# Layer 0 of a four-layer cross-attention stack: keys and values by pairs of batches, scores by seven products of halves

## The chip, the core and the metric

The kernel runs on one core of a Trainium2 chip. The core has a matrix engine (TensorE, PE), a vector engine (VectorE, DVE), a scalar engine for activations (ScalarE, ACT), a general engine (GpSimd, POOL) and a sync engine (SyncE, SP), which here only issues DMAs. Each engine works through its own queue in order; semaphores tie them together. TensorE reads from SBUF and writes to PSUM, which has eight banks of 512 fp32 columns; GpSimd doesn't read PSUM in this kernel. PEld in a profile is the loading of TensorE's weights, which runs beside its matmuls. The metric is the device time of one execution in microseconds (us), the median of several runs.

## The reference

Four layers work on `x` of shape (4, 512, 512) with a context of shape (4, 64, 512): four batches `b`, 512 tokens, 512 channels. All is fp32. Layer 0, which most of the change concerns, is this (cut, names shortened; it has 16 heads of 128, and both attentions read the same context):

```python
def attention(q_in, ctx, wq, bq, wk, bk, wv, bv, wo, bo, bias_k, bias_v):
    qh = (q_in @ wq + bq).reshape(b, 512, 16, 128)
    kh = (ctx @ wk + bk).reshape(b, 64, 16, 128)
    vh = (ctx @ wv + bv).reshape(b, 64, 16, 128)
    kh = concatenate([kh, broadcast(bias_k)], axis=1)      # 65 keys
    vh = concatenate([vh, broadcast(bias_v)], axis=1)
    weights = softmax(einsum('bqhk,bthk->bhqt', qh, kh) / sqrt(128))
    return einsum('bhqt,bthk->bqhk', weights, vh).reshape(b, 512, 2048) @ wo + bo

x = x + attention(layer_norm(x, ln1), ctx, ...1)
x = x + attention(layer_norm(x, ln2), ctx, ...2)
h = layer_norm(x, ln_mlp)
x = x + gelu(h @ w_fc1 + b_fc1) @ w_fc2 + b_fc2            # 512 -> 2048 -> 512
```

Layer 1 is a small cross-attention. Layer 2 attends over its own 512 tokens and the 64 of the context (16 heads of 32), with an RMS norm and an MLP behind it. Layer 3 is a layer norm, a cross-attention over the context, a second layer norm and an MLP.

## The kernel before

**A plan makes the order.** The kernel doesn't issue its instructions as it describes them. Each `with pe(...)`, `dve(...)`, `act(...)`, `pool(...)`, `either(...)` or `load(...)` records one operation with an estimated cost for each engine that may do it; `either` allows ScalarE or VectorE, and `added` allows VectorE or GpSimd. `Plan.order` first merges streams that were declared to run side by side (`beside`) by their shares of TensorE time, then walks through time: each free engine takes the earliest recorded operation that is ready and has room in SBUF and PSUM, at most 150 us of TensorE work ahead of the oldest open operation (`AHEAD`; 60 us for loads). What it chooses becomes the fixed order of each engine's queue. Its estimates (`t_dve`, `t_act`, `t_pool`, `MM`, `TR`, and in `load` 5.0 us for each 2048 elements of a partition, in `attempt` 0.1 us for an issue on SP) decide this order; on the chip each instruction takes what it takes.

SBUF is one tile, "arena", PSUM one tile, "banks"; all buffers are cut from these two, so a profile names hardly anything else. Helpers record many operations under one line: `mm4` (L693) is any group of four matmuls, the evictions of `either` are at L546 and L547 (`move`), L551 and L552 (`shift`), L555 and L556 (`affine`), additions between SBUF buffers at L925 (`added`).

**Layer 0.** For each of its two attentions (`n`) and each half of the 16 heads (`half`), `l0_project` reads the weights of eight heads, four loads of 256 KB a head, and makes for all four batches at once: the keys `kT` and the values `vT` (L693, 256 context tokens wide), then `A`, the query weights times the keys (L788, 4 x 65 = 260 columns, `KW`), `cq`, the query bias times the keys (L794), and `U`, the values times the output weights (L807). The queries themselves are never made: the scores are the normalized tokens times `A`. Bias rows are made at L820 and L838.

`normed` makes the layer norm: statistics on VectorE (L712, L713), a square root on ScalarE (L718), the normalization itself on GpSimd (L725), transposes on TensorE (L734), and scale and offset as `affine`. `l0_attention` then takes one batch in four tiles of 128 tokens. A tile's scores for eight heads are eight matmuls of 128 x 260 (two banks); VectorE adds `cq` (L862), finds the maximum (L870) and subtracts it (L872), ScalarE takes the exponential (L874), VectorE sums (L877) and inverts (L879), GpSimd scales (L882, L884), TensorE transposes (L893) and multiplies by `U` (four matmuls 512 wide), and VectorE adds the result to `x` (L901). After the second half of the heads the bias rows are added (L906 to L917). L1656 adds the output bias row to `x` on GpSimd.

The loop over layer 0 takes `n`, then the first half for all four batches with the norm of each, then the second half for all four.

**The later layers.** Two batches at a time, an MLP (`mlp`) is declared beside the attention of another layer or pair, so that the plan mixes the two. The MLP already multiplies by seven products of halves instead of eight (`seven`, L963, with `moving_sums` and `stationary_sums`), as do projections of layers 2 and 3 (`token_sums`, `seven_halves`, L1241). `layer_norm` and `mean_of` (layer 3, and the RMS norm of layer 2) have their sums over channel chunks and the last product on GpSimd (L1312, L1341, L1344, L1357), a mean by a matmul (L1315, L1347), and a reciprocal of 3.3 us on VectorE (L1323).

Of the kernel before, what the change touches and what calls it, by code (L numbers as in the profile page):

```python
# [14 lines left out]
ALU = mybir.AluOpType  # L15
# [3 lines left out]
P = 128  # L19
# [9 lines left out]
KW = B * (T + 1)  # L29
F = 2048  # L30
# [166 lines left out]
class Plan:  # L197
# [174 lines left out]
    def attempt(self, narrow):  # L372
# [22 lines left out]
        while left:  # L395
            progress = True
            while progress:
# [8 lines left out]
                for e, heap in heaps.items():  # L406
# [58 lines left out]
                    if op.load:  # L465
                        free_at[e] = now + 0.1
                        dma_free = max(dma_free, now) + cost
                        end = max(dma_free, now) + 2.0
                        busy[e] += cost
                    else:  # L470
                        free_at[e] = end = now + cost
                        busy[e] += cost
                        heapq.heappush(events, (end, 0, -1))
# [144 lines left out]
def stack(nc, const, sbuf, psum, a, out):  # L618
# [56 lines left out]
    def load(view, src, n):  # L675
        with pl.op(load=True, SP=n / 2048 * 5.0) as o:
            o.dma_start(out=view, in_=src)
# [28 lines left out]
    def normed(src, scale, offset):  # L706
# [7 lines left out]
        rstd = sb(NT)  # L714
# [4 lines left out]
        with dve(4) as o:  # L719
            o.reciprocal(rstd.v(), rstd.v())  # L720
        xn = []
        for t in range(NT):
            n = sb(D)
            with pl.op(POOL=2.1) as o:
                o.tensor_scalar(  # L725
                    n.v(), src[t].v(), mv.v(NT, 2)[:, t, 0:1], rstd[:, t : t + 1], ALU.subtract, ALU.mult
                )
            xn.append(n)
# [15 lines left out]

    bias = {}

    def l0_project(n, half):
        A = [sb(HH * KW) for _ in range(NC)]
        cq = sb(HH * KW)
        U = [sb(HH // 2 * D) for _ in range(B)]  # L750
        if not half:

            bvd = sb(H * DH)
            with pool(512) as o:
                o.memset(bvd.v(), 0.0)
            for g in range(4):
                with pool(4) as o:
                    o.tensor_copy(
                        bvd[:, g * 129 : g * 129 + 109 : 36], col(f"L0_xattn_bias_v{n}")[:, 4 * g : 4 * g + 4]
                    )  # L760
            bias[n] = [bvd, sb(D), None]
        bvd, ub, _ = bias[n]
        vTs, wos = [], []
        for j in range(HH):
            h = half * HH + j
            heads = slice(h * P, (h + 1) * P)

            wk = loaded(chunks(a[f"L0_wk{n}"][:, heads]), NC, P)
            wq = loaded(a[f"L0_wqT{n}"][heads, :], D)
            kT = sb(KW)  # L770
            p = ps()
            with pe(4 * MM[256]) as o:
                mm4(o, p[:, : B * T], lambda c: wk.v(NC, P)[:, c, :], lambda c: ctxT[:, c, :])
            with either(256) as o:
                o.shift(kT.v(B, T + 1)[:, :, :T].k(0), p[:, : B * T].split(B, T), col(f"L0_xattn_bk{n}", h))
            with pool(1) as o:
                o.tensor_copy(kT.v(B, T + 1)[:, :, T].k(1), col(f"L0_xattn_bias_k{n}", h).to_broadcast([P, B]))
            wv = loaded(chunks(a[f"L0_wv{n}"][:, heads]), NC, P)
            vT = sb(B * T)
            p = ps()  # L780
            with pe(4 * MM[256]) as o:
                mm4(o, p[:, : B * T], lambda c: wv.v(NC, P)[:, c, :], lambda c: ctxT[:, c, :])
            with either(256) as o:
                o.shift(vT.v(), p[:, : B * T], col(f"L0_xattn_bv{n}", h))
            for c in range(NC):
                p = ps()
                with pe(MM[KW]) as o:
                    o.matmul(p[:, :KW], wq[:, c * P : (c + 1) * P], kT.v(), start=True, stop=True)  # L788
                with either(KW) as o:
                    o.move(A[c].v(HH, KW)[:, j, :].k(j), p[:, :KW])  # L790

            p = ps()
            with pe(MM[KW]) as o:
                o.matmul(  # L794
                    p[:, :KW], col(f"L0_xattn_bq{n}", h).to_broadcast([P, P]), kT.v(), start=True, stop=True
                )
            with either(KW) as o:
                o.move(cq.v(HH, KW)[:, j, :].k(j), p[:, :KW])
            wo = loaded(a[f"L0_wo{n}"][heads, :], D)
            vTs.append(vT)  # L800
            wos.append(wo)
            if j % 2:
                for b in range(B):
                    p = ps()
                    with pe(PAIR) as o:
                        for e in range(2):
                            o.matmul(  # L807
                                p[e * T : (e + 1) * T, :],
                                vTs[j - 1 + e][:, b * T : (b + 1) * T],
# [4 lines left out]
                    with either(D) as o:  # L814
                        o.move(U[b].v(HH // 2, D)[:, j // 2, :].k(j // 2), p.v())
            if j % 4 == 3:
# [16 lines left out]
        if half:  # L833
# [3 lines left out]
            with pe(MM[512]) as o:  # L837
                o.matmul(p.v(), fold, ub.v(), start=True, stop=True)  # L838
# [3 lines left out]
        return A, cq, U  # L842

    def l0_attention(n, half, b, hT, proj, pb):
        qs = 1.0 / math.sqrt(P)
        A, cq, U = proj
        for t in range(NT):

            p = ps(2)
            own = slice(b * (T + 1), (b + 1) * (T + 1))  # L850
            with pe(8 * MM[KW]) as o:
                for i in range(2):
                    mm4(
                        o,
                        p.v(2, 512)[:, i, :KW],
                        lambda c: hT[c][:, t * P : (t + 1) * P],
                        lambda c: A[c].v(HH, KW)[:, 4 * i : 4 * i + 4, own],
                    )
            sc = sb(HH * (T + 1))
            s3 = sc.v(HH, T + 1)  # L860
            with dve(520) as o:
                o.tensor_tensor(  # L862
                    sc.v(2, 4, T + 1),
                    p.v(2, 512)[:, :, :KW].arrange("p i (h s) -> p i h s", h=4),
                    cq.v(2, 4, KW)[:, :, :, own],
                    ALU.add,
                )
            m = sb(HH)
            with dve(520) as o:
                o.tensor_reduce(m.v(), s3, AX.X, ALU.max)  # L870
            with dve(520) as o:
                o.tensor_tensor(s3, s3, m.v().new(2).bc(P, HH, T + 1), ALU.subtract)  # L872
            with act(520, "exp") as o:
                o.activation(sc.v(), sc.v(), AF.Exp, scale=qs)  # L874
            r = sb(HH)
            with dve(520) as o:
                o.tensor_reduce(r.v(), s3, AX.X, ALU.add)  # L877
            with dve(8) as o:
                o.reciprocal(r.v(), r.v())  # L879
            pr = sb(HH * T)  # L880
            with pool(512) as o:
                o.tensor_tensor(pr.v(HH, T), s3[:, :, :T], r.v().new(2).bc(P, HH, T), ALU.mult)  # L882
            with pool(8) as o:
                o.tensor_tensor(  # L884
                    pb.v(NT, 2, 4, 4)[:, t, 0].arrange("p i g -> p g i")[:, 2 * half : 2 * half + 2, :].k((t, half)),
                    s3[:, :, T].arrange("p (g i) -> p g i", g=2),
                    r.v(2, 4),
                    ALU.mult,
                )
            p = ps()  # L890
            with pe(4 * TR) as o:
                for k in range(HH // 2):
                    o.transpose(p[:, k * P : (k + 1) * P], pr[:, k * P : (k + 1) * P], ident)  # L893
            prT = sb(HH * T)
            with either(512) as o:
                o.move(prT.v(), p.v())
            p = ps()
            with pe(4 * MM[512]) as o:
                mm4(o, p.v(), lambda k: prT[:, k * P : (k + 1) * P], lambda k: U[b].v(HH // 2, D)[:, k, :])
            with dve(512) as o:  # L900
                o.tensor_tensor(x[b][t].v(), p.v(), x[b][t].v(), ALU.add)  # L901
        if half:
# [12 lines left out]
            for t in range(NT):  # L915
                with dve(512) as o:
                    o.tensor_tensor(x[b][t].v(), banks[t].v(), x[b][t].v(), ALU.add)  # L917

# [389 lines left out]
    def mean_of(parts):  # L1308

        for i, j in ((0, 1), (2, 3), (0, 2)):  # L1310
            with pool(S) as o:
                o.tensor_tensor(parts[i].v(), parts[i].v(), parts[j].v(), ALU.add)  # L1312
# [22 lines left out]
    def layer_norm(src, scale, offset):  # L1335

        parts = []
        for i in range(2):
            t = sb(S)
            with pool(S) as o:  # L1340
                o.tensor_tensor(t.v(), src[2 * i].v(), src[2 * i + 1].v(), ALU.add)  # L1341
            parts.append(t)
        with pool(S) as o:
            o.tensor_tensor(parts[0].v(), parts[0].v(), parts[1].v(), ALU.add)  # L1344
# [10 lines left out]
        for c in range(NC):  # L1355
            with pool(S) as o:
                o.tensor_tensor(xc[c].v(), xc[c].v(), r.v(), ALU.mult)  # L1357
# [288 lines left out]
    for n in (1, 2):  # L1646
        hT, pb = [], []
        proj = l0_project(n, 0)
        row = load_row(f"L0_xattn_bo{n}")
        for b in range(B):  # L1650
            if n == 1:
                load_x(b)
            hT.append(normed(x[b], f"L0_xattn_ln{n}_scale", f"L0_xattn_ln{n}_offset"))
            for t in range(NT):
                with pool(512) as o:
                    o.tensor_tensor(x[b][t].v(), x[b][t].v(), row.v(), ALU.add)  # L1656
# [115 lines left out]
```

## Time and profile before

| | |
|---|---|
| median of 3 runs (lowest, highest) | 2810.38 us (2808.79, 2812.26) |
| the profiled execution: its time, its span | 2809.43 us, 2807.7 us |
| mean granted TensorE clock in it | 0.996 |
| TensorE idle in the span | 66 us |
| matmul records at L963 (MLPs): count, busy | 2688, 1214.6 us |
| records of the scores of layer 0 (128x260 at L693): count, busy | 1024, 232.8 us |
| records of keys and values from the context (128x256 at L693, all layers): count, busy | 640, 151.8 us |
| L725 on GpSimd: count, busy, mean | 48, 100.0 us, 2092 ns |
| loads of 256 KB of layer 0 weights: issue to landing | 3.1 to 3.8 us |
| HBM read, written | 123.52 MB, 4.19 MB |

A row of a profile's group list gives the line, the engine, the operation, what is written and read, the shape and the count, then the busy time, the mean of one instruction, and the idle time of the engine just before them with what ended it. A busy time is a union of spans, and a matmul's end is modelled, so it holds a little more than the engine's bare work. In a timeline a row begins with its start and its length; the last number of a row of waits is the longest one.

### The profile page before, as it was taken

Reading aid. Unit: us, or ns where it says so; the run is one execution under the profiler, and the core shown is the slowest. Engines: PE = TensorE matmul, PEld = TensorE weight load, DVE = VectorE, ACT = ScalarE, POOL = GpSimd, SP = SyncE. Lnnn points to the kernel's source line nnn. Section 1 sums busy time; section 2 is a strip of 40 time slices with the busy share of each in tenths; the row PEclk is TensorE's granted clock in tenths of the full one; section 3 lists DMA queues with packets and bytes.
Section 4 is the critical chain, followed back from the end, with each engine's and each line's share of the span. In section 5 each row is a group of like instructions: output and inputs, shape, how many; then the busy total and the mean of one; then the engine's idle time right before and its main releaser. Section 6 shows DMA issues by size and latency. Waiting matters only on the chain. (4 is left out here: it accounts for less than half of the span.)

```text
span 2807.7 us, 31089 instructions
## 1 busy us (share of the span) xinstructions
PE 2741.5 (98%) x10924; PEld 1566.2 (56%) x10924; DVE 1905.9 (68%) x3344; ACT 825.1 (29%) x1503; POOL 1073.0 (38%) x1136
## 2 busy tenths in 40 slices
PE   8999999999999999999999999999999989999999
PEld 6666666766655455555555655555454535454444
DVE  5646556556655577777786877778875878687655
ACT  1310112101221113552562355245332323232311
POOL 2720125301542352324335232423744556455521
PEclk9999999999999999999999999999999999999999
DMA  5112021120111120120102012011111111102210
GB/s 166 31 57 71 19 64 35 57 64 23 38 43 59 45 68 9 31 61 16 38 31 79 9 31 73 18 31 42 42 45 46 46 49 42 45 16 67 75 38 30
DMA packets 186523, 129.72 MB, mean 46 GB/s; under 512 B 6992, under 2 KB 163280, under 8 KB 186368
## 3 DMA queue, kind: packets, MB, share of 16 engines
q1 hardware_dynamic: 186000, 127.43, 15.0%
q8 instruction: 87, 1.43, 0.2%
q14 instruction: 68, 0.56, 0.1%
q0 software_dynamic: 80, 0.16, 0.0%
q10 hardware_dynamic: 288, 0.15, 0.0%
HBM read 123.52 MB, written 4.19 MB: 45 GB/s over the span
## 5 line engine op out<-in xcount | busy, mean ns | idle before, releaser
L963 PE MATMUL banks<-arena 128*128 128x512 f32 x2688 | 1214.6, 597 | 16.0 <-DVE arena L982 9.2
L925 POOL TENSOR_TENSOR arena<-arena 128x256 f32<-128x256 f32 (+1 forms) x579 | 597.8, 1046 | 658.7 <-DVE arena L547 108.9
L963 PEld LDWEIGHTS banks<-arena 128*128 128x128 f32 x2688 | 499.0, 191 | 593.2 <-issue 503.7
L693 PE MATMUL banks<-arena 128*128 128x260 f32 (+3 forms) x1968 | 598.4, 459 | 3.0 <-ACT arena L555 1.1
L693 PEld LDWEIGHTS banks<-arena 128*128 128x128 f32 x1968 | 358.5, 189 | 212.4 <-issue 169.7
L546 ACT COPY arena<-banks 128x512 f32<-128x512 f32 (+3 forms) x403 | 209.8, 543 | 751.8 <-PE banks L963 218.2
L925 DVE TENSOR_TENSOR arena<-arena 128x256 f32<-128x256 f32 (+1 forms) x465 | 374.4, 819 | 49.4 <-ACT arena L998 19.1
L547 DVE COPY arena<-banks 128x512 f32<-128x512 f32 (+3 forms) x513 | 292.4, 576 | 157.8 <-PE banks L963 48.0
L998 ACT ACTIVATE arena<-arena,cols 128x512 f32<-128x512 f32 x192 | 137.4, 721 | 394.9 <-DVE arena L982 175.3
L982 DVE TENSOR_TENSOR arena<-banks,arena 128x512 f32<-128x512 f32 x240 | 164.7, 686 | 120.5 <-PE banks L963 108.6
L882 POOL TENSOR_TENSOR arena<-arena 128x512 f32<-128x512 f32 x64 | 71.8, 1122 | 388.5 <-DVE arena L879 348.9
L1241 PE MATMUL banks<-arena 128*128 128x256 f32 x896 | 206.3, 380 | 2.6 <-DVE arena L982 1.0
L1470 ACT ACTIVATE arena<-banks,arena 128x512 f32<-128x512 f32 x256 | 174.7, 687 | 82.0 <-DVE arena L1460 38.6
L1241 PEld LDWEIGHTS banks<-arena 128*128 128x128 f32 x896 | 168.6, 190 | 54.1 <-issue 21.6
L1458 DVE TENSOR_REDUCE arena<-banks 128x1 f32<-128x512 f32 x256 | 167.3, 680 | 13.5 <-PE banks L1447 11.8
L1504 PEld LDWEIGHTS banks<-ident,arena 128*128 128x128 f32 x1024 | 115.3, 141 | 82.3 <-ACT arena L1470 30.2
L693 PE MATMUL banks<-ctxT,arena 128*128 128x256 f32 x640 | 151.8, 388 | 7.8 <-DMA arena<-in_L_wk 7.3
L1504 PE MATMUL banks<-ident,arena 128*128 128x128 f32 x1024 | 138.5, 276 | 9.6 <-ACT arena L1470 8.9
L693 PEld LDWEIGHTS banks<-ctxT,arena 128*128 128x128 f32 x640 | 121.9, 193 | 40.2 <-issue 12.7
L1021 DVE TENSOR_TENSOR arena<-banks,arena 128x512 f32<-128x512 f32 x144 | 98.4, 685 | 49.8 <-PE banks L963 49.4
L725 POOL TENSOR_SCALAR arena<-arena 128x512 f32<-128x512 f32 x48 | 100.0, 2092 | 30.6 <-DVE arena L720 12.4
L1481 POOL TENSOR_TENSOR arena<-arena 128x256 f32<-128x256 f32 x64 | 39.5, 617 | 187.1 <-DVE arena L1460 121.2
(152 smaller groups left out, 2437.6 us busy)
## 6 DMA issues: line engine op xcount, KB each, us to landing
arena<-in_L_w SPq DMA_DIRECT2D x192, 256.0 KB, 3.2
arena<-in_L_wk SPq DMA_DIRECT2D x48, 256.0 KB, 3.3
arena<-in_L_wqT SPq DMA_DIRECT2D x32, 256.0 KB, 3.7
arena<-in_L_wv SPq DMA_DIRECT2D x32, 256.0 KB, 3.6
arena<-in_L_wo SPq DMA_DIRECT2D x32, 256.0 KB, 3.1
arena<-in_L_wq SPq DMA_DIRECT2D x32, 256.0 KB, 3.8
arena<-in_L_wo SPq DMA_DIRECT2D x8, 1024.0 KB, 5.5
arena<-in_L_wv SPq DMA_DIRECT2D x6, 1024.0 KB, 7.3
```

Source lines behind the costliest of these rows:

```text
L546: "ACT": lambda e, out, in_: e.copy(out, in_),
L547: "DVE": lambda e, out, in_: e.tensor_copy(out, in_),
L693: o.matmul(dst, lhs(c), rhs(c), start=(c == 0), stop=(c == NC - 1))
L725: o.tensor_scalar(n.v(), src[t].v(), mv.v(NT, 2)[:, t, 0:1], rstd[:, t : t + 1], ALU.subtract, ALU.mult)
L925: o.tensor_tensor(out, x, y, op)
L963: o.matmul(p.v(), lhs(c), rhs(c), start=(c == 0), stop=(c == 1))
L982: o.tensor_tensor(t.v(), p.v(), y.v(), ALU.add)
L998: o.activation(g[f].v(), src.v(), func, bias=col(b1, q * NC + f))
L1241: o.matmul(p[:, i * 256 : (i + 1) * 256], lhs(c), rhs(c), start=(c == 0), stop=(c == 1))
L1458: o.tensor_reduce(m[:, i : i + 1].k(i), banks[i].v(), AX.X, ALU.max)
L1470: o.activation(y.v(), banks[i].v(), AF.Exp, bias=nm[:, i : i + 1].k(i), scale=qs, accum_out=sums[:, i : i + 1].k(i),)
L1504: o.transpose(p[:, c * P : (c + 1) * P], e[i][:, c * P : (c + 1) * P], ident)
```

## The change

- `l0_project` becomes `l0_keys` and `l0_values`, declared side by side, and both work for one pair of batches (`bp`; 128 context tokens, `KP` = 130 columns of keys). Each is therefore called for each pair, and each call loads the weights of its eight heads.
- The loop over layer 0 takes the pair first, then `n`, then the half of the heads. In the first half both batches of the pair are normed, then the output bias row is added to both, and then both are attended to.
- The scores of two tiles (tokens `m` and `2 + m` of the four) and eight heads are a product of 2 x 2 blocks: token halves by channel halves by head halves. It is made of seven block products instead of eight. `token_sums` makes the sums of the left side from the normed tokens, `l0_keys` those of the right side (`t1` to `t4`) and of the bias (`dcq`), and VectorE or GpSimd puts the blocks together. What follows for one tile is the new `l0_tile`, unchanged but for the subtraction of the maximum, which may now go to VectorE or GpSimd.
- In `normed` the normalization is a scale and an offset (`by`, one more small instruction) on ScalarE or VectorE instead of GpSimd.
- In `mean_of` and `layer_norm` the sums and the product on GpSimd may now go to VectorE or GpSimd (`added`).
- The plan's figure for a load is 3.15 instead of 5.0 us for 2048 elements, and an issue on SP is counted as 0.45 instead of 0.1 us.

```diff
-                        free_at[e] = now + 0.1
+                        free_at[e] = now + 0.45
...
-        with pl.op(load=True, SP=n / 2048 * 5.0) as o:
+        with pl.op(load=True, SP=n / 2048 * 3.15) as o:
...
+        with dve(4) as o:
+            o.scalar_tensor_tensor(by.v(), mv.v(NT, 2)[:, :, 0], -1.0, rstd.v(), ALU.mult, ALU.mult)
...
-            with pl.op(POOL=2.1) as o:
-                o.tensor_scalar(
-                    n.v(), src[t].v(), mv.v(NT, 2)[:, t, 0:1], rstd[:, t : t + 1], ALU.subtract, ALU.mult
-                )
+            with either(D) as o:
+                o.affine(n.v(), src[t].v(), rstd[:, t : t + 1], by[:, t : t + 1])
...
+    def l0_keys(n, half, bp):
+        tokens = slice(bp * P, (bp + 1) * P)
+        b11, b21, b22, t1, t2, t3, t4 = (sb(2 * 4 * KP).v(2, 4, KP) for _ in range(7))
+        cq, dcq = (sb(4 * KP).v(4, KP) for _ in range(2))
+        for j in range(4):
+            for e in range(2):
+                h = half * HH + 4 * e + j
+                heads = slice(h * P, (h + 1) * P)
+                wk = loaded(chunks(a[f"L0_wk{n}"][:, heads]), NC, P)
+                wq = loaded(a[f"L0_wqT{n}"][heads, :], D)
+                kT = sb(KP)
+                p = ps()
+                with pe(8 * TR) as o:
+                    mm4(o, p[:, :P], lambda c: wk.v(NC, P)[:, c, :], lambda c: ctxT[:, c, tokens])
...
+                made = []
+                for r in range(2):
+                    p = ps()
+                    with pe(4 * TR) as o:
+                        for c in range(2):
+                            o.matmul(p[:, c * KP : (c + 1) * KP], wq[:, (2 * r + c) * P : (2 * r + c + 1) * P], kT.v(), start=True, stop=True)
+                    made.append(p[:, : 2 * KP].split(2, KP))
...
+                if not e:
+                    for dst, p4 in ((b11, made[0]), (b21, made[1])):
+                        with either(2 * KP) as o:
+                            o.move(own(dst), p4)
...
+                with dve(2 * KP) as o:
+                    o.tensor_tensor(own(t1), own(b11), made[0], ALU.subtract)
+                with either(2 * KP) as o:
+                    o.move(own(b22), made[1])
+                with dve(2 * KP) as o:
+                    o.tensor_tensor(own(t3), own(b22), made[0], ALU.add)
+                added(own(t2), own(b22), own(t1), ALU.subtract, 2 * KP)
+                added(own(t4), own(b21), own(t2), ALU.subtract, 2 * KP)
...
+    def l0_attention(n, half, b, X, keys, U, pb):
+        for m in range(2):
...
+            u1 = plus(some(), product(a11, b11), cq[:, :, own])
+            u2 = plus(some(), product(s2, t2), u1)
+            u3 = plus(some(), product(s3, t3), u2)
+            p5 = plus(some(), product(s1, t1), dcq[:, :, own])
+            u4 = some()
+            added(u4, p5, u2, ALU.add, 2 * KP)
+            added(c22, p5, u3, ALU.add, 2 * KP)
+            plus(c11, product(a12, b21), u1)
+            plus(c21, product(a22, t4), u3)
+            plus(c12, product(s4, b22), u4)
+            for t, sc in ((m, scs[0]), (2 + m, scs[1])):
+                l0_tile(half, b, t, sc, U, pb, qs)
...
-            with pool(S) as o:
-                o.tensor_tensor(xc[c].v(), xc[c].v(), r.v(), ALU.mult)
+            added(xc[c].v(), xc[c].v(), r.v(), ALU.mult, S)
...
+    for bp, pair in enumerate(pairs):
+        for n in (1, 2):
+            X, pb = {}, {}
+            for half in range(2):
+                made = {}
+                pl.beside(
+                    lambda: made.update(keys=l0_keys(n, half, bp)), lambda: made.update(U=l0_values(n, half, bp))
+                )
+                if not half:
+                    row = load_row(f"L0_xattn_bo{n}")
+                    for b in pair:
+                        if n == 1:
+                            load_x(b)
+                        X[b] = token_sums(normed(x[b], f"L0_xattn_ln{n}_scale", f"L0_xattn_ln{n}_offset"))
...
+                for b in pair:
+                    l0_attention(n, half, b, X[b], made["keys"], made["U"], pb[b])
```

In `l0_attention` a `product` is two matmuls of 128 x 260 into one bank, and `plus` adds such a bank and a buffer on VectorE. `l0_values` makes `vT` (128 tokens), `U` for two batches and, for the first pair only, the bias rows, as before.

## The prediction, made before the changed kernel ran

> **What bounds the kernel now.** I read the busy shares first, then the busy times by stage, then the waits of TensorE, and last the timeline for single prices.
>
> ```profile
> PE 2741.5 (98%) x10924; PEld 1566.2 (56%) x10924; DVE 1905.9 (68%) x3344; ACT 825.1 (29%) x1503; POOL 1073.0 (38%) x1136
> ...
> 0.00:780.00 780.00, 769.62 (x3261) 518.28 (x3262) 453.28 (x854) 135.75 (x213) 240.86 (x279) 1.00 0.19 56
> 780.00:2808.00 2028.00, 1971.90 (x7665) 1047.94 (x7663) 1452.60 (x2491) 689.35 (x1291) 832.12 (x858) 0.99 0.14 42
> ...
> PE banks L693 <- DMA arena<-in_L_wk: 7.3, 1, 7.3
> PE banks L693 <- ACT arena L555: 1.1, 1, 1.1
> PE banks L693 <- DVE arena L556: 1.1, 1, 1.1
> PE banks L693 <- DVE arena L552: 0.6, 1, 0.6
> ```
>
> The columns of the two stage rows are TensorE, weight load, VectorE, ScalarE and GpSimd busy, then granted clock, DMA share and GB/s. Layer 0 is the first 780 us. TensorE is busy for 769.6 of them at full clock; the four waits below the rows are nearly all it waits for there, and 7.3 of them are the first load. So layer 0 costs what its matmuls cost, VectorE (58%) and GpSimd (31%) have room, and an edit counts by the TensorE time it removes or the waits it makes. After 780 us TensorE is idle for 56 us.
>
> **Prices.** Busy times overlap at the seams, so I take the distance from start to start in the timeline. An fp32 matmul leaves two records (the scores are 512 matmuls and 1024 records), a transpose one.
>
> ```profile
> 33.10 3.62 PE L693 MATMUL banks<-ctxT,arena 128*128 128x256 f32 x16
> 36.55 1.92 PE L788 MATMUL banks<-arena 128*128 128x260 f32 x8
> 38.30 0.60 PE L794 MATMUL banks<-arena,cols 128*128 128x260 f32 x2
> ...
> 92.18 0.60 PE L893 MATMUL banks<-ident,arena 128*128 128x128 f32 x4
> 92.62 1.54 PE L734 MATMUL banks<-ident,arena 128*128 128x128 f32 x12
> ...
> 1019.96 2.79 PE L693 MATMUL banks<-arena 128*128 128x64 f32 x24
> 1022.58 0.65 PE L963 MATMUL banks<-arena 128*128 128x512 f32 x1
> ```
>
> Eight matmuls 256 wide take 3.45 us (0.431 each), four 260 wide 1.75 (0.4375), twelve 64 wide 2.62 (0.218), four transposes 128 wide 0.44 (0.11 for one record).
>
> **The change, part by part.**
>
> Scores. Before: 64 tiles of 8 matmuls 260 wide, 512. After: 32 pairs of tiles with seven products of two, 448. The built order of the changed kernel has 448 too. 64 x 0.4375 = **28.0 us off TensorE**, nothing else of it being on the path.
>
> Keys and values by pairs of batches. 256 matmuls 256 wide become 512 that are 128 wide; the 128 + 32 of A and cq (260) become 256 + 64 that are 130 wide. The columns are the same, the instructions twice as many. No fp32 matmul of 128 columns is in this trace. Lower bound: half of the 256-wide one, 0.2156, which costs nothing more. Upper bound: the straight line from 64 (0.218) to 256 (0.431), 0.289 at 128 and 0.291 at 130, since a cost that is flat and then rises lies under its chord: 512 x 0.289 - 110.3 = 37.7, and 320 x 0.291 - 70.0 = 23.1, together +60.8. I take two records of 0.109, because the 64-wide matmul shows that a record with its weight load can't go below that, and the 128-wide transposes show that 128 columns with a weight load need no more: 512 x 0.2185 - 110.3 = +1.6 and 320 x 0.222 - 70.0 = +1.0, **+2.6 us**. The U products, bias rows and all transposes keep their number (the bias rows are made for the first pair only).
>
> Against this stands a page of the Trainium skill, "TensorE: Matmul & The Clock Gate", section "Back-to-back issue gap": a real stream of weight load and matmul at 128 columns is said to sustain about 81 ns each, where columns alone would give 56, a surcharge of some 45%. As an estimate from that page, 832 narrow matmuls would pay about 82 us more, and the sum would end near 2870. The row of 64-wide matmuls, each with its 128 x 128 weights, speaks against it.
>
> VectorE and GpSimd in layer 0. For a pair of tiles the old 2 x 0.696 (L862) becomes seven additions out of PSUM of 260 elements, 0.418 each by L1253 (256 wide): +1.53 us. Two sums of 260 in SBUF and the two subtractions of the maximum (0.780, L872) may now go to either engine. So a pair of tiles holds VectorE for 7 x 0.418 + 2 x (0.689 + 0.690 + 0.197 + 0.690) = 7.5 us, and 11.8 if it also took all that could go elsewhere (2 x 0.707, 2 x 0.780, 2 x 0.688 of moves). TensorE needs 14 x 0.4375 + 8 x 0.11 + 8 x 0.858 = 13.9. Projection: two heads take TensorE 16 x 0.2185 + 10 x 0.222, and 2 x 0.96 for U (four such pairs took 3.84 us, L807): 7.6 us, with the bias rows of the first pair 8.2. Moves, shifts, differences and sums take 6.6 us if VectorE does all. Both fit; value **0** while the planner's order keeps products ahead, and what it costs if that cover is gone is in the second rival. Token sums of layer 0 (64 additions of 256, 0.71 to 0.80) go beside attention. By the built order's counts VectorE gains about 41 us in layer 0 (453 to 494 of some 755) and GpSimd about 105.
>
> LayerNorm, `normed`. 48 GpSimd steps of 2.09 us become ScalarE or VectorE steps of about 0.72 to 0.81 (L998, L556); one small instruction is added for each. ScalarE is 17% busy in layer 0 (136 of 780), so the exponentials queued behind them wait little. On the path they stand only where a stage starts, in the two waits of 1.1 us: the first product stands at the head of TensorE's queue, and all that follows waits with it. There are now four such starts (two pairs, two attentions), and eight sums stand behind the last transposes. Three of the seven products need none of the sums, and in the built order 38 to 42 matmuls follow the transposes without a break. I take 1.5 us for each start, bounds 0.5 and 3: 4 x 1.5 - 2.2 = **+4** (0 to +10). The additions of the output bias (L1656) now stand behind both norms of a pair on GpSimd, and only the residual additions (L901) at the end of a tile need them.
>
> LayerNorm of layer 3 (`mean_of`, `layer_norm`): 92 GpSimd steps of 1.36 to 1.42 us may go to VectorE. Where such a norm is exposed, both engines are full:
>
> ```profile
> 2003.00:2044.00 41.00, 35.02 (x81) 15.26 (x80) 39.00 (x40) 19.26 (x26) 38.44 (x36) 0.92 0.00 1
> 2303.00:2331.00 28.00, 18.85 (x36) 7.43 (x35) 26.81 (x26) 13.69 (x19) 25.34 (x21) 0.82 0.00 0
> ```
>
> TensorE loses 15.1 us there, with a lower granted clock, but VectorE and GpSimd are over 90% busy, so moving a step between them frees little: **-1**. At best half of the 15 goes (-8); at worst steps of 0.945 us stand on VectorE ahead of the L982 that TensorE waits for, five times (+5).
>
> Loads. The 128 weight loads of layer 0 are issued twice: 33.5 MB and 128 issues on SP more. From 10 to 30 us the DMA engines moved 334 to 344 GB/s, all they do here. One stage's 32 loads are 8.39 MB, 24.7 us at 339 GB/s, under the 4 x 7.6 = 31 us of projection; an issue took 0.43 to 0.55 us, 16 for the 32. TensorE waited for a load once, before the first. Value **0**, nothing to gain, worst case in the third rival. The planner's new figures (0.79 us for 256 KB, an issue of 0.45) move no work by themselves; they reorder all later layers, where 56 us are idle: 0, and I allow 10 either way.
>
> Sum: -28.0 + 2.6 + 4 - 1 = -22.4 on the profiled execution's 2809.43 (span 2807.7), 2787.0. The median of the runs shown is 0.95 above that execution: **2788 us**. The forecast's own range takes the starts at 0 and +10, layer 3 at -8 and +5, and 5 us either way for the order: 2772 to 2805.
>
> **Rivals.**
> 1. Narrow matmuls pay for their weights. At the chord the sum is 2810.4 - 28.0 + 60.8 + 3 = 2846. It turns to a loss from (180.3 + 25) / 832 = 0.247 us each. Against it: the 64-wide row. Chance 0.04.
> 2. Stage starts take the gain back, slower than before. Behind the last tile of a pair stand statistics (4 x 0.87), a table load and root (1.28 + 0.2 and three small steps, 0.7), four normalizations on two engines (1.5), transposes (1.75), affine (0.8) and sums three deep (2.1): 11.8 us. Open at all four starts, with 2.2 known, that is +45 and 2829; it decides from (26.4 + 2.2) / 4 = 7.2 us a start. For it: a pair has half the other work that four batches had. Against it: 31 us of projection is independent and stands ahead of the transposes in the built order. Chance 0.08.
> 3. Loads come late: each of the seven later stages waits for one landing (3.1 to 3.8 us by the list of DMA issues), +24, so about 2812: no change. For it: buffers are shared, and SP already waits for them. Chance 0.10.
> 4. The later layers gain too: the 8 us of layer 3 and 10 from the new order, 2771. Chance 0.10.
> 5. That the products aren't fewer is excluded by the built order.
>
> **How the numbers follow.** The forecast has 0.68. Differences under 0.2%, 5.6 us, can't be told from none: faster is 0.68 + 0.10 = 0.78, within 0.2% 0.10, slower 0.12. The range 2768 to 2812 leaves out rivals 1 and 2 and a little at the lower end.
>
> **What would show it.** Scores 448 matmuls at 0.4375 from start to start and key matmuls near 0.219; layer 0 over near 758 us instead of 780; gaps before the first products of four stages of 1 to 3 us; VectorE in layer 0 near 65%. Wrong would be: 128-wide matmuls over 0.247, waits for DMA beyond the first one, or layers 1 to 3 shifted by more than 10 us.

## The result and the profile after

The changed kernel took a median of 2821.18 us (2819.88 to 2826.01, 5 runs) against 2810.05 us (2808.79 to 2812.26, 5 runs): ratio 1.0043, 95% interval 1.0029 to 1.0058. The forecast was 2788. The profiled execution took 2821.01 us with a span of 2819.2, 11.5 more than before.

Busy shares of the changed kernel, then its busy times by stage, with the columns as before:

```profile
PE 2742.9 (97%) x11628; PEld 1578.9 (56%) x11628; DVE 1968.8 (70%) x3569; ACT 885.8 (31%) x1659; POOL 1095.0 (39%) x1277
```

```profile
0.00:780.00 780.00, 764.01 (x3938) 525.61 (x3939) 496.51 (x1051) 194.54 (x371) 280.14 (x423) 1.00 0.33 100
780.00:2819.00 2039.00, 1978.85 (x7693) 1053.26 (x7691) 1472.29 (x2519) 691.28 (x1289) 814.82 (x854) 0.99 0.14 42
```

TensorE is as busy as before (2742.9 us against 2741.5), though 64 score matmuls are gone. The waits of TensorE in the changed kernel show little of where that went: between 25 and 760 us they come to 6.9 us, against 2.4 before. The longest of all and the longest of layer 0:

```profile
PE banks L1031 <- ACT arena L1423: 12.3, 2, 9.5
PE banks L694 <- DMA arena<-in_L_wk: 7.4, 1, 7.4
PE banks L977 <- ACT arena L547: 1.8, 3, 0.8
PE banks L785 <- DVE arena L553: 1.3, 1, 1.3
PE banks L735 <- ACT arena L552: 1.1, 1, 1.1
```

(L1031 is the product of the MLPs. From here on, layer 0 means its two attentions; its MLP counts with the later layers.) So I matched each record of TensorE with the operation that it belongs to, added up the distances from start to start, and charged what goes beyond the usual distance of a form to the record that came late. Split by the layer for which the work is done, the wait for the first load with layer 0:

| | layer 0 | later layers | span |
|---|---|---|---|
| before | 767.1 | 2040.6 | 2807.7 |
| changed | 768.9 (+1.8) | 2050.3 (+9.7) | 2819.2 |

Two things are to be explained: a layer 0 that gained nothing, and later layers that lost 9.7 us with hardly a change in their arithmetic.

**Where layer 0's gain went.** The timeline of TensorE in the kernel before, where a projection ends:

```profile
36.55 1.92 PE L788 MATMUL banks<-arena 128*128 128x260 f32 x8
...
38.84 3.84 PE L807 MATMUL banks<-arena 128*64 128x512 f32 x16
42.61 1.07 PE L820 MATMUL banks<-arena 128*32 128x512 f32 x8
43.60 2.64 PE L693 MATMUL banks<-ctxT,arena 128*128 128x256 f32 x11
```

and the same kind of place in the changed kernel (L785 is A, L694 keys and values, L796 `cq`, L850 U):

```profile
327.23 1.05 PE L694 MATMUL banks<-ctxT,arena 128*128 128x128 f32 x8
328.12 0.39 PE L796 MATMUL banks<-arena,cols 128*128 128x130 f32 x2
328.34 1.05 PE L694 MATMUL banks<-ctxT,arena 128*128 128x128 f32 x8
329.33 1.08 PE L850 MATMUL banks<-arena 128*64 128x512 f32 x4
330.34 1.16 PE L785 MATMUL banks<-arena 128*128 128x130 f32 x8
331.43 1.08 PE L850 MATMUL banks<-arena 128*64 128x512 f32 x4
332.44 0.49 PE L796 MATMUL banks<-arena,cols 128*128 128x130 f32 x2
```

The U products use 64 columns of the array (128*64). Before, 16 of their records stand in a row; now four stand alone between full 128*128 matmuls. Read the starts: eight key records take 0.89 us (327.23 to 328.12), but 0.99 when U follows (328.34 to 329.33); the eight A records between two U groups take 1.09. In layer 0 an entry costs 93 ns nearly every time, whether operands and bank had been ready for 140 ns or for over 2 us; the first and the last pair of U records take 480 and 529 ns instead of 430, and the matmul behind the last one comes 103 ns late. A visit to a narrow tile thus costs about 0.35 us beyond its work (of U's 128 pairs 64 took 430 ns before, and 10 after). None of it is idle time in the profile, since the modelled ends overlap. Between 25 and 760 us there were 22 visits before and 70 after. The Trainium skill has the rule in "TensorEngine Tiling (Array Packing)", section "Key Properties": changing the tiling mode drains TensorE. The traces agree that the change costs time and give it a size, which the page doesn't; that it is a drain they don't show.

The accounts of layer 0, before to changed, from distances from start to start:

| term | us |
|---|---|
| scores: 225.0 to 201.0 | -24.0 |
| keys, values, A and `cq`, by the usual distance of a group | +5.6 |
| 48 more visits, entry and exit: 48 x (93 + 103) ns | +9.4 |
| U's own records: 60.2 to 64.1 | +3.9 |
| groups that start less than 200 ns after their bank (or operand) came free: 36 before, losing 4.4 us; 48 after, losing 13.9 (a few are entries too, and those behind a score, 1.5 us more than before, are in the scores' row as well) | +9.5 |
| transposes of the attentions' norms: 17.1 to 15.1 | -2.0 |
| sum (measured: +1.8) | +2.4 |

### The profile page after: what moved, and what is told of

The parts are those of the page before. It is cut to its first block, busy times and chain, and to the rows that moved or that the text cites. A ratio compares the mean times of both kernels' runs of the same rounds, so it can differ in the third digit from the quotient of the medians.

```text
span 2819.2 us, 33561 instructions
## 1 busy us (share of the span) xinstructions
PE 2742.9 (97%) x11628; PEld 1578.9 (56%) x11628; DVE 1968.8 (70%) x3569; ACT 885.8 (31%) x1659; POOL 1095.0 (39%) x1277
## 5 line engine op out<-in xcount | busy, mean ns | idle before, releaser
L993 POOL TENSOR_TENSOR arena<-arena 128x256 f32<-128x256 f32 (+3 forms) x828 | 840.0, 1030 | 1119.9 <-ACT arena L547 202.3
L1031 PE MATMUL banks<-arena 128*128 128x512 f32 x2688 | 1212.9, 597 | 18.2 <-ACT arena L1423 12.3
L1031 PEld LDWEIGHTS banks<-arena 128*128 128x128 f32 x2688 | 499.7, 191 | 594.9 <-issue 509.6
L993 DVE TENSOR_TENSOR arena<-arena 128x512 f32<-128x512 f32 (+3 forms) x564 | 449.8, 813 | 69.7 <-ACT arena L1066 16.2
L547 ACT COPY arena<-banks 128x512 f32<-128x512 f32 (+4 forms) x464 | 227.5, 511 | 786.4 <-PE banks L1031 215.6
L548 DVE COPY arena<-banks 128x512 f32<-128x512 f32 (+2 forms) x420 | 253.7, 613 | 189.0 <-PE banks L1031 43.9
L694 PE MATMUL banks<-arena 128*128 128x512 f32 (+2 forms) x944 | 371.1, 542 | 2.3 <-DVE arena L548 0.9
L694 PEld LDWEIGHTS banks<-arena 128*128 128x128 f32 x944 | 167.8, 190 | 180.1 <-issue 167.5
L1050 DVE TENSOR_TENSOR arena<-banks,arena 128x512 f32<-128x512 f32 x240 | 164.4, 686 | 104.1 <-PE banks L1031 94.6
L906 PE MATMUL banks<-arena 128*128 128x260 f32 x896 | 208.5, 384 | 0.8 <-ACT arena L547 0.7
L1309 PEld LDWEIGHTS banks<-arena 128*128 128x128 f32 x896 | 170.0, 191 | 54.8 <-issue 23.2
L906 PEld LDWEIGHTS banks<-arena 128*128 128x128 f32 x896 | 164.7, 188 | 38.4 <-issue 5.8
L694 PE MATMUL banks<-ctxT,arena 128*128 128x128 f32 (+1 forms) x1152 | 164.1, 291 | 8.8 <-DMA arena<-in_L_wk 7.4
L694 PEld LDWEIGHTS banks<-ctxT,arena 128*128 128x128 f32 x1152 | 148.5, 194 | 27.5 <-issue 13.6
L1568 PE MATMUL banks<-ident,arena 128*128 128x128 f32 x1024 | 140.6, 278 | 12.1 <-ACT arena L1534 11.5
L1089 DVE TENSOR_TENSOR arena<-banks,arena 128x512 f32<-128x512 f32 x144 | 98.7, 686 | 46.0 <-PE banks L1031 45.7
L985 DVE TENSOR_TENSOR arena<-banks,arena 128x512 f32<-128x512 f32 x64 | 44.2, 690 | 117.0 <-PE banks L694 114.1
```

The lines of the kernel that those rows point to most:

```text
L547: "ACT": lambda e, out, in_: e.copy(out, in_),
L548: "DVE": lambda e, out, in_: e.tensor_copy(out, in_),
L694: o.matmul(dst, lhs(c), rhs(c), start=(c == 0), stop=(c == NC - 1))
L906: o.matmul(p[:, : 2 * KP], lhs(c), rhs(c, b % 2), start=(c == 0), stop=(c == 1))
L993: o.tensor_tensor(out, x, y, op)
L1031: o.matmul(p.v(), lhs(c), rhs(c), start=(c == 0), stop=(c == 1))
```

## The experiments

"Layer 0" and "later" are the sums explained above, from each run's profiled execution; that of e7 is 5.7 us longer than its median, that of e9 6.1 shorter. All ratios are to the kernel before.

| run | median us | ratio, 95% interval | layer 0 | later |
|---|---|---|---|---|
| e1_figures | 2834.89 | 1.0089 (1.0072, 1.0105) | 789.0 | 2044.2 |
| e2_norms | 2810.57 | 1.0006 (0.9997, 1.0016) | 770.4 | 2039.8 |
| e3_pairs8 | 2836.69 | 1.0099 (1.0084, 1.0114) | 791.4 | 2043.7 |
| e4_oldfig | 2822.08 | 1.0046 (1.0031, 1.0061) | 785.0 | 2035.0 |
| e5_oldest_bank | 2801.32 | 0.9967 (0.9954, 0.9979) | 765.7 | 2033.8 |
| e6_oldest_bank_before | 2784.18 | 0.9908 (0.9895, 0.9922) | 758.2 | 2024.1 |
| e7_slack | 2813.91 | 1.0018 (1.0008, 1.0027) | 769.7 | 2048.2 |
| e8_ahead140 | 2816.49 | 1.0024 (1.0014, 1.0034) | 768.5 | 2046.0 |
| e9_u_in_fours | 2812.00 | 1.0007 (0.9998, 1.0015) | 758.5 | 2045.7 |
| e10_fours_oldest | 2786.41 | 0.9921 (0.9908, 0.9935) | 755.9 | 2031.9 |
| e11_twos_oldest | 2788.14 | 0.9923 (0.9910, 0.9935) | 753.6 | 2030.4 |
| e12_ln3_gpsimd | 2816.52 | 1.0026 (1.0014, 1.0038) | 768.7 | 2045.7 |
| e13_figures_layer0 | 2805.79 | 0.9986 (0.9977, 0.9994) | 769.4 | 2035.7 |
| e14_twos_oldest_fig0 | 2780.38 | 0.9896 (0.9882, 0.9909) | 754.6 | 2023.5 |
| e15_e14_ln3_gpsimd | 2784.86 | 0.9919 (0.9906, 0.9933) | 753.1 | 2030.0 |
| e16_issue_kept | 2805.65 | 0.9986 (0.9977, 0.9995) | 769.1 | 2034.4 |
| e17_load_kept | 2822.13 | 1.0046 (1.0034, 1.0059) | 769.3 | 2051.5 |

### The change in parts

**e1: the figures alone**, in the kernel before.

```diff
-                        free_at[e] = now + 0.1
+                        free_at[e] = now + 0.45
...
-        with pl.op(load=True, SP=n / 2048 * 5.0) as o:
+        with pl.op(load=True, SP=n / 2048 * 3.15) as o:
```

> The kernel before with the plan's two new DMA figures alone (0.45 us for an issue on SP, 3.15 us for 2048 elements). Where the two traces are laid beside each other, the changed kernel is 1.3 us late at the end of layer 0 and 11.5 us late at the end, so about 10 us went to layers whose arithmetic was hardly changed. Theory A (the new figures reorder the later layers for the worse): 2818 to 2822. Rival B (the LayerNorm steps that may go to VectorE do it): within 3 us of 2810. Rival C (neither; it comes from how layer 0 hands over to the later layers): within 3 us of 2810 too, told from B by the next run.

25.6 us slower, more than any theory had, and 21.9 of them in layer 0: the other order makes 59 groups there wait for a bank or operand just freed (28.1 us). In part of that time TensorE's own clock was lower; of two such stretches, the number before the last two is the granted clock:

```profile
506.00:512.00 6.00, 4.42 (x9) 2.13 (x10) 3.07 (x7) 3.99 (x5) 5.82 (x6) 0.72 0.01 3
636.00:650.00 14.00, 10.76 (x23) 5.92 (x24) 4.37 (x10) 1.48 (x4) 0.00 (x0) 0.62 0.25 76
```

Only 3.6 us came in the later layers. Two figures in a planner cost more than all arithmetic of the change saves.

**e2: the LayerNorm edits alone**, in the kernel before.

```diff
-            with pl.op(POOL=2.1) as o:
+            with either(D) as o:
...
-            with pool(S) as o:
-                o.tensor_tensor(xc[c].v(), xc[c].v(), r.v(), ALU.mult)
+            added(xc[c].v(), xc[c].v(), r.v(), ALU.mult, S)
```

> The kernel before with the edits of the LayerNorms alone (normalization on ScalarE or VectorE with the extra small instruction, sums and last product of layer 3 on VectorE or GpSimd). Rival B: 2816 to 2822, lost behind 1000 us. Theory A and rival C: within 3 us of 2810. My prediction's own step for it (stage starts of layer 0 not counted) was -1, -8 to +5: 2802 to 2815.

No difference that can be measured; rival B falls for the kernel before.

**e3: pairs of batches, but eight products.**

```diff
-            u1 = plus(some(), product(a11, b11), cq[:, :, own])
...
+            p = ps(2)
+            with pe(8 * MM[KW]) as o:
+                for i in range(2):
+                    mm4(o, p.v(2, 512)[:, i, :KW], lambda c: hT[c][:, t * P : (t + 1) * P], lambda c: Ar[c // 2][:, c % 2, 4 * i : 4 * i + 4, own])
```

> The changed kernel with the scores by eight products of 128x260 again (512 matmuls, one addition of the bias product in two banks, as before), but still by pairs of batches, with the loads made twice, the new norms and the new figures. What layer 0 pays for working in pairs stands here without the seven products. Theory (the seven products do save 24 to 28 us, and pairs cost that much: 64 matmuls at 0.4375 come back): 2845 to 2850, layer 0 about 24 us longer than in the changed kernel. Rival (the chain of seven products with its additions on VectorE makes the stalls, and pairs cost only 6 us of narrower matmuls): 2816 to 2826.

Between the two, because the later layers are 6.6 us shorter than in the changed kernel; layer 0 is 24.3 us longer than before and 22.5 longer than with seven products. The seven products do bring what they take off TensorE, and working in pairs costs as much. By the same distances, each counted once, the 24.3 us are the entries and exits of its 72 visits (10.3) and U's records (4.1), narrow matmuls (5.7), scores of 222 instead of 219 ns a record (3.1), late starts behind a full tile (1.7) and a small rest.

Part of the rival holds: starts behind a full tile that come more than 15 ns late (a count a little narrower than that of the table) lose 5.5 us between 25 and 760 us here, 4.1 before and 12.9 in the changed kernel. So the late starts come with the seven products, or with the order planned for them, and not with the pairs.

**e4: the changed kernel with the old figures.** The two lines of e1 the other way round.

> The changed kernel with the plan's old DMA figures (0.1 and 5.0 us). Theory A (the figures cost the later layers about 10 us): 2809 to 2813, with the time at the end of layer 0 unchanged within 3 us. Rivals B and C: within 3 us of 2821.

The time is the same, as B and C had it, but its parts aren't, and no theory had that: layer 0 is 16.1 us longer, the later layers 15.3 shorter. Of the 16.1, 7.4 are a single wait of TensorE for a norm at the start of a stage:

```profile
PE banks L735 <- ACT arena L556: 7.7, 2, 7.4
```

In the changed kernel the new figures help layer 0, where they cost the kernel before 21.9 us, and hurt behind it.

### Banks

A bank of PSUM that is wanted was dealt out by the lowest free address, often the one emptied last.

```diff
-        at = min(self.free[size])
+        _, at, start, size = min(
+            (max(self.given.get(c, 0) for c in range(at, at + buf.size, 512)), at, start, size)
+            for size, starts in self.free.items() if size >= buf.size
+            for start in starts for at in range(start, start + size, buf.size))
```

(`given` holds when a bank was last given back.) **e5** does this in the changed kernel, whose order stays the same on every engine, **e6** in the kernel before.

> The changed kernel with its order of instructions unchanged on every engine; only the PSUM banks are dealt out otherwise: the bank that has been free longest, instead of the lowest address. In the changed kernel's trace, of the groups of matmuls of layer 0 that follow a full 128x128 group, 48 start less than 200 ns after VectorE or ScalarE has emptied the bank (or made the operand) that they need, nearly all of them a bank, and lose about 14 us; in the kernel before 36, with 4.4 us. Theory P (the planner hands a bank to the next product in the moment in which its plan empties it, and on the chip the emptying is a little late): 2806 to 2813, nearly all of it in layer 0. Rival D (the evictions themselves are late, whichever bank it is, or the operands): 2818 to 2824.

> The kernel before with the same rule for PSUM banks. Control: it has a third of the bank waits in layer 0 (4.4 us against 14), so theory P gives it 2 to 6 us: 2804 to 2808. Rival D: within 3 us of 2810.

The rule is worth 20 and 26 us, but not where I expected it: 16.5 us in the later layers of both, and in layer 0 only 3.2 for the changed kernel against 8.9 for the one before. Behind 780 us TensorE's idle time fell from 56 us before (2028.00 less 1971.90 in the stage row) to 40 in e6:

```profile
780.00:2782.00 2002.00, 1962.07 (x7639) 1050.82 (x7637) 1448.18 (x2480) 685.14 (x1285) 825.38 (x852) 1.00 0.14 43
```

One wait of TensorE there, at the scores of layer 2, before:

```profile
PE banks L1447 <- ACT arena L1470: 8.9, 9, 2.2
```

and with the oldest bank (e6, lines moved by 23):

```profile
PE banks L1470 <- ACT arena L1493: 2.4, 4, 1.2
```

So theory P holds in kind for the kernel as a whole, with more than it forecast, and falls as the explanation of layer 0. There the late starts of the changed kernel fell from 12.9 to 9.4 us. The many small ones went; eight of 0.3 to 1.3 us, 7.0 in all, still follow within 150 ns on VectorE or ScalarE emptying the bank. For these, where even the bank that has been free longest was emptied only just before, rival D fits: the evictions themselves are late.

### More slack, and another order for nothing

**e7** and **e8**, in the changed kernel:

```diff
-    AFTER_PE, AFTER, BEFORE_PE = 0.2, 0.06, 0.1
+    AFTER_PE, AFTER, BEFORE_PE = 0.25, 0.1, 0.15
...
-AHEAD, AHEAD_LOAD, RESERVE = 150.0, 60.0, 4
+AHEAD, AHEAD_LOAD, RESERVE = 140.0, 60.0, 4
```

> The changed kernel with more time between dependent operations in the plan (0.25 us after TensorE, 0.10 after other engines and 0.15 before TensorE, for 0.20, 0.06 and 0.10). Theory P has it that the plan is cut too fine: layer 0 with 8 to 15 us fewer waits than the 32.5 above the usual spacing of its matmuls, but the order changes everywhere, and the later layers may go either way by 8: 2803 to 2820. Rival D: layer 0 as long as in the changed kernel, 2815 to 2830.

> The changed kernel planned with a horizon of 140 us of TensorE work instead of 150: an edit without a meaning of its own, which only deals out another order. It measures how far the order alone scatters the time. From the six orders seen so far, the later layers took 2035 to 2050 us whatever was edited: I expect 2812 to 2830, with the later layers between 2035 and 2050. If the 9.7 us of the changed kernel in the later layers came from its LayerNorm edits and not from the lot of the order, they stay: later layers 2048 to 2052.

Slack did nothing for layer 0 (769.7), against theory P. A meaningless edit moved the median by 4.7 us: a difference of a few us between two plans says nothing of an edit's worth.

### The visits

**e9**: four U groups as one operation in four banks (**e11**: two in two banks).

```diff
-            if j % 2:
-                for i in range(2):
-                    p = ps()
-                    with pe(PAIR) as o:
+            if j % 4 == 3:
+                banks = [(g, i, ps()) for g in (j - 3, j - 1) for i in range(2)]
+                with pe(4 * PAIR) as o:
+                    for g, i, p in banks:
```

> The changed kernel with the U products (value times output weight, 64 columns of TensorE each) of four heads and two batches as one operation in four banks, so that they follow each other on TensorE. In every trace so far each step of TensorE from a full 128x128 group to one of 64 or 32 columns or rows costs 93 ns, and the way back 45 + 103 ns, whatever had been ready how long: 0.24 us a visit. Layer 0 has 22 such visits between 25 and 760 us in the kernel before and 70 in the changed one; by the plan's order 24, 73 and, here, 31. Theory S (the visits are what the pairs of batches cost): 42 fewer, 10 us; layer 0 757 to 761 us instead of 768.9 by the sum of its matmuls' distances. Rival N (narrow matmuls and late evictions, not the visits): layer 0 within 3 us of 768.9. The later layers fall as the order does, 2035 to 2050: in all 2794 to 2811, or 2806 to 2822 with N.

Layer 0 fell by 10.4 us, as theory S had it, with 29 visits; its profiled execution is the shortest of 11 runs, and the median lies 1 us above the range. TensorE's timeline of e9:

```profile
320.89 1.95 PE L694 MATMUL banks<-ctxT,arena 128*128 128x128 f32 x16
322.77 3.65 PE L850 MATMUL banks<-arena 128*64 128x512 f32 x16
326.35 1.16 PE L785 MATMUL banks<-arena 128*128 128x130 f32 x8
327.35 0.39 PE L796 MATMUL banks<-arena,cols 128*128 128x130 f32 x2
```

Sixteen U records take 3.58 us (322.77 to 326.35), where four alone took 1.01. U's records fell from 64.1 to 57.3 us, and 41 fewer entries and exits are another 8.0; of these 14.8, 4.4 went back, 2.3 of them into waits for banks (13.9 to 16.2). My 0.24 us a visit in the expectation left out what a visit costs inside U's own records.

> The same with the PSUM bank that has been free longest, as in the run that took the changed kernel to 2801. Theory S: layer 0 of 765.7 falls by 10 to 753 to 758 us, and the bank rule keeps its 16 us in the later layers: 2778 to 2796, so that it may pass the kernel before with that rule (2784). Rival N: 2798 to 2806.

> U products of two heads and two batches as one operation in two banks, with the oldest free bank. 48 visits in the plan's order, 25 fewer than in the changed kernel: theory S gives 6 us, layer 0 758 to 762 us; rival N 763 to 769. In all 2784 to 2800 by S.

Layer 0 came 9.8 and 12.1 us below that of e5. With twos it is under the expected range though it has more visits (45), since it waits less: late starts behind full tiles lose 6.6 us, against 13.3 with fours (e10). Rival N falls in both.

### The later layers

**e12**: the changed kernel with `mean_of` and `layer_norm` as before the change. **e13**: the new figures for layer 0 alone. **e14**: e13 with the oldest bank and the U groups in twos. **e15**: e14 with the edit of e12. **e16** and **e17** are e13 with one new figure kept behind layer 0.

```diff
-                        free_at[e] = now + 0.45
+                        free_at[e] = now + (0.45 if op.n < self.first else 0.1)
...
-        with pl.op(load=True, SP=n / 2048 * 3.15) as o:
+        with pl.op(load=True, SP=n / 2048 * (3.15 if pl.first == 1 << 30 else 5.0)) as o:
...
+    pl.first = len(pl.ops)
     h = {}
```

> The changed kernel with the sums and the product of the later LayerNorms on GpSimd alone, as before. If these edits cost the later layers their 9.7 us, they are back at 2038 to 2043 and the kernel at 2809 to 2814. If it is the lot of the order, the later layers lie anywhere from 2035 to 2050; between 2044 and 2052 would be against the edits as the cause.

> The changed kernel with the new DMA figures for the loads of layer 0 alone and the old ones behind it, so that the order of layer 0 stays as it is and the later layers are planned as before. Theory F (the new figures cost the later layers their 9.7 us, as the 2035 of the run with the old figures everywhere suggests): later layers 2034 to 2042, in all 2803 to 2812. Rival L (the lot of any new order): later layers anywhere from 2035 to 2050; 2044 to 2050 speaks for L.

> The same with the U products in twos and the oldest free bank: layer 0 as in the run without the old figures (753 to 757). Theory F: the later layers fall from 2030 to 2016 to 2024, in all 2770 to 2782, under the 2784 of the kernel before with the oldest bank. Rival L: 2024 to 2034, in all 2778 to 2791.

> That kernel with the sums and the product of the later LayerNorms on GpSimd alone, as before the change. Taken from the changed kernel alone, this edit gave 4.6 us in the later layers. If that was the edit, 3 to 6 us less than the run above; if it was the lot, anything within 8 us of it on either side.

> The changed kernel; behind layer 0 the plan counts a load with the old 5.0 us for 2048 elements, an issue with the new 0.45 us. If the new issue figure is what costs the later layers (SP's queue is then planned as the narrow place, so loads and the work on them are chosen in another order), they stay at 2044 to 2050 and the kernel at 2814 to 2821; if it is the load figure, 2034 to 2042 and 2803 to 2812.

> The changed kernel; behind layer 0 the plan counts an issue with the old 0.1 us, a load with the new 3.15 us for 2048 elements. The mirror of the run above: if the load figure costs the later layers, 2044 to 2050 (2814 to 2821); if the issue figure does, 2034 to 2042 (2803 to 2812). If both runs end at the same place, the two figures cannot be told apart from the lot of the order.

e13 leaves layer 0 alone and takes 14.6 us off the later layers; e16 does the same and e17 nothing: it is the load figure, 3.15 for 5.0 us. In the kernel before, both new figures together cost the later layers 3.6 us (e1), so the size goes with the order that they meet. One wait of TensorE that differs, in e17 and then in e16 (a LayerNorm of layer 3 ahead of an MLP):

```profile
PE banks L1032 <- ACT arena L1424: 12.3, 2, 9.6
```

```profile
PE banks L1032 <- ACT arena L1424: 1.9, 2, 1.2
```

With the lowest bank, every run with the new load figure behind layer 0 has later layers of 2043.7 to 2051.5 us (eight runs with the changed kernel), and every one with the old 2034.4 to 2040.6 (five runs with the kernel before); the two don't overlap. That the wait above is the way in which it happens is not shown: e2 and e4 have a wait of 9.5 us there too, with the old figure. e12 and e15 give the edit of the LayerNorms opposite signs (4.6 us shorter without it, 6.5 longer), so its worth is not settled and not above the scatter of orders.

e14 is the fastest version, its busy shares:

```profile
PE 2727.5 (98%) x11628; PEld 1588.6 (57%) x11628; DVE 1950.6 (70%) x3544; ACT 892.8 (32%) x1683; POOL 1093.6 (39%) x1271
```

It and e6, the kernel before with nothing but the bank rule, are both about 1% faster than the kernel before; their intervals overlap, so which of the two is better isn't settled.

## Why the prediction was wrong

- Scores, -28.0: right in kind, -24.0 in size. A record took 222 ns instead of 219, and with waits a matmul 0.449 us (201.0 / 448) instead of 0.4375. The 222 ns came in e3 too, where the scores are products of four as before; what makes them isn't shown.
- Narrow matmuls, +2.6: right in kind, +5.6. The usual group of four keys took 0.893 us, 0.223 a matmul, and A 0.2245. The chord (0.289) didn't come, nor did the 82 us estimated from the Trainium skill, "TensorE: Matmul & The Clock Gate", section "Back-to-back issue gap"; rival 1 needed 0.247.
- "The U products ... keep their number": this is the step that failed in layer 0. They did, and were valued at nothing for it; but their neighbours changed. 48 more visits cost 13.3 us (9.4 around them, 3.9 within), and e9, with 41 fewer, gave 10.4 back. Nothing in my reading asked how often TensorE changes its tile, though the trace of before had the price at each of its 22 visits.
- VectorE and GpSimd in layer 0, 0: failed too. The cover that I named, products ahead of the sums, held for long waits and not for short ones: 9.5 us in 100 ns pieces and a few of 1 us. The prediction left the price of a lost cover to rival 2, which counts only the starts of stages. What causes the late starts is only partly shown: they come with the seven products and their order (e3), and the oldest bank took 3.2 us off.
- Stage starts, +4, and rival 2: wrong in sign; the transposes of the norms took 2.0 us less. Such a start can be dear all the same: 7.4 us with the old figures (e4).
- Loads, 0, and rival 3: right. Landings rose to 4.8 to 5.5 us, and no wait but the first was for a load.
- LayerNorm of layer 3, -1: no size can be told (e2, e12, e15).
- The planner's figures, 0 (10 either way): the step that failed in the later layers. The load figure costs 14.6 us there (e13), more than the 10 I allowed, and the forecast's range took only 5 of these; rival 4 had the other sign.

Of the signs that the prediction named for being wrong, none came: key matmuls took 0.223 us, under 0.247, only the first load was waited for, and the later layers shifted by 9.7 us, under 10. What failed was not on its list.

## What to carry to other kernels

When work is cut into smaller batches, count not only its matmuls but how often TensorE changes between full and narrow tiles, and keep the narrow groups together. Deal out PSUM banks by how long they have been free, before tuning anything finer. In a planned kernel test each figure of the plan alone, and take no difference for an edit's worth that a meaningless change of order makes as well.

## What was not expected of the hardware

- A visit to a 64-column tile between full tiles: 93 ns before it, 50 and 99 ns on its first and last pair of records, 103 ns behind it; no idle time shows.
- In the first stretch of matmuls, from 7.3 to about 15 us, a record of a key product takes 213 ns instead of 112 in the changed kernel, and 427 instead of 216 before; it costs both nearly 4 us beside their waits. The granted clock reads 1.00 there in the profile. In e1 a record 512 wide takes 853 ns instead of 429 between 509 and 512 us, and there the granted clock does read lower (0.72 from 506 to 512).
